# An attention layer and a bottleneck block in one kernel: other places for the residual's transfers, the weights' preparation and VectorE's share

## The chip, the cores and the metric

The kernel runs on one core of one Trainium2 chip. The metric is the device time of one execution in microseconds (us). A core has TensorE (PE), VectorE (DVE), ScalarE (ACT), GpSimd (POOL) and SyncE (SP). In the trace each engine runs its instructions in the order in which the program gives them to it. DMA transfers are issued on SP and on POOL here.

## The reference

The input x is (4, 1024, 32, 32) in float32: four images of 1024 channels and 1024 places. Layer 0 is attention with 16 heads of 64, layer 1 a bottleneck of three convolutions with batch norms.

```
x0 = tokens(x)                                    # (4, 1024, 1024)
q, k, v = split(x0 @ w_qkv.T + b_qkv)
q, k = rmsnorm(rope_2d(q)), rmsnorm(rope_2d(k))   # over all 1024 features
ctx = softmax(q @ k.T / 8) @ v                    # per head
x1 = rmsnorm(ctx @ w_proj.T) + x0                 # the residual
h = relu(bn(conv1x1(x1)))                         # 1024 -> 256
h = relu(bn(conv3x3(h)))                          # 256 -> 256
out = relu(x1 + softplus(s) * bn(conv1x1(h)))     # 256 -> 1024
```

## The kernel before

Everything is in float32. The images go through layer 0 one after another: projections q, k and v, attention, projection y. Layer 1 follows.

**Projections.** A 1024 x 1024 projection is a Strassen-like product (Winograd's form): seven products of halves instead of eight. Image 0 does this once (`project`, 28 steps); its operands are sums of weight blocks that `operands` makes on VectorE while TensorE works (L236 to L239: tiles such as w_v_1b) and stores to DRAM (wd, L242). Images 1 to 3, and y of all images, do it twice over (`project2`): seven outer products of seven inner ones, 49 weight tiles of 256 KB each, loaded on SP (L398, L465) into the ring wring of eight tiles. Their inner operands are sums of sums. `prepare` makes them once: four loads, four VectorE operations (L407 to L410), and four stores on POOL to wd2 (L412). A part is one of the seven outer products of one projection; there are 28 parts, and four block steps for y (`prepare_blocks`). Each part of q, k and v must be stored by the time image 1 projects, each of y by y of image 0.

**Where a part is prepared.** `weight_parts(parts, first, step, lag, alloc)` begins part i at `first + i * step` products from now, with its loads on POOL, and makes its sums `lag` products later. `alloc` gives room: pieces of a tile not yet in use (`pieces_of`), or `big_pieces`, which takes two tiles of the pool big (three tiles of 128 x 1024). Other parts are prepared in the attention of image 0: `extra_step` makes the sums of one part and loads the next, once per pair of heads, with loads on SP into wring. Before the change q of image 0 carries seven parts, k five, v none, attention the four block steps, y's seven parts and k's parts 2 to 6, and v's parts 2 to 5 are begun during y of image 0.

**Rope and norm.** `rope` turns q (and k) after its projection. The reciprocal norms are multiplied into the tables cosT and sinT (L722), and each of eight turns (L728 to L732) does two VectorE operations of 128 x 1024: one into a tile of big (qs or ks), one in place. Two accumulating transfers on POOL (L734) add the first into the second. The last turn reloads the tables (L169 to L172, on SP).

**Order.** For TensorE, VectorE, ScalarE and POOL the order is that in which the program issues, so a Python clock spreads VectorE's side work. Each product adds its share to `pace["room"]`; each piece of side work spends its cost in units of TT, VectorE's time for one operation of 128 x 512 as a share of a product. While room is left, `product_done` issues the next of `waiting`. A turn costs four TT. At the end of v `rest(leave=4)` leaves up to four turns in `waiting`, and attention issues one per pair. SP's order is found by a scheduler.

**Attention.** For each half c of the queries and each of eight pairs of heads: scores (L791), exponentials on ScalarE (L798), their sums over keys on VectorE (L800, L802), products with v (L808). Every second pair VectorE takes reciprocals (L835), which SP spreads (L838 and after), and POOL adds v's bias (L772). The tile probs_ holds one pair's exponentials.

**Residual.** `o_norm` writes the normed y to x1d in DRAM (L852). The residual is then added to x1d by eight accumulating transfers of 128 x 1024 on POOL (L1052) per image, issued all at once just before the next image's attention (for images 0 to 2; image 3 adds it on VectorE). x1d is read back after the last attention.

Of the kernel before, what the change touches and what calls it, by code (L numbers as in the profile page):

```python
# [13 lines left out]
ALU = mybir.AluOpType  # L14
# [4 lines left out]
P = 128  # L19
B, C, H, W = 4, 1024, 32, 32  # L20
N = H * W
NT = C // P
# [12 lines left out]
WQ, WK, WV, WP, W1 = 0, NFB, 2 * NFB, 3 * NFB, 4 * NFB  # L35
# [30 lines left out]
OUTER = ("A11", "A12", "S2", "S3", "S1", "S4", "A22")  # L66
# [19 lines left out]
def program(ctx, tc, x, wblk, w2, w3, vecs, cos, sin, out, bad):  # L86


    nc = tc.nc
# [6 lines left out]
    x1d = dram.tile([NT, P, B * N], F32, name=f"x1d{u}")  # L96
# [56 lines left out]
    with tc.tile_pool(name=f"st{u}", bufs=2) as st, ExitStack() as s:  # L153
# [70 lines left out]
        def operands(b, base, g, name):  # L224
# [14 lines left out]
            nc.vector.tensor_tensor(a12, a12, a11, ALU.subtract)  # L239
            spend(4 * TT)  # L240
            for o, t in enumerate((a11, s1, a21, a12)):
# [2 lines left out]

        TT = 0.19
        later, waiting = [], deque()
        pace = {"at": 0, "room": 0.0, "hold": False, "tables": 0.0}

        def spend(cost):
            pace["room"] -= cost
# [379 lines left out]
        def v_proj(b, bs, ts, v, two=None):  # L632

            if two is not None:
                project2(b, 1, WV, *two, v, True, "v", lambda c: None)
                return

            def outs(g):
                n = N // P // 2
                return [  # L640
                    v[:, c * n : (c + 1) * n, f * P : (f + 1) * P] for f in (g, g + NG) for c in range(NCH)
                ]

            project(b, WV, bs, ts, outs, None, lambda *a, **k: None, True, "v")
# [126 lines left out]
            nc.vector.tensor_tensor(cx, cx, w, ALU.mult)  # L771
            nc.gpsimd.tensor_scalar(cx, cx, col("bv", hp), None, ALU.add)  # L772

        def attention(b, c, q_all, k_all, v, probs_, late, ready, extra):


            at = half[c]
            sums_ = []
            for hp in range(NHP):
                n = f"{b}_{c}_{hp}"  # L780
                if late:
                    late.pop(0)()
                rows = shifts(q_all, k_all, n, hp, c) if bad is None else None
                probs = []
                d_ = acc.tile([P, 2, CH], F32, tag="tot", name=f"den_{n}")
                for t in range(N // P):
                    p = probs_[:, t]
                    sc = bank("sc", f"sc_{n}_{t}")
                    for j in range(2):
                        d = slice(j * HD, (j + 1) * HD)  # L790
                        nc.tensor.matmul(  # L791
                            sc[:, j], k_all[d, hp, t * P : (t + 1) * P], q_all[d, hp, at],
                            start=True, stop=bad is not None,
                        )
                    if bad is None:
                        for j in range(2):
                            nc.tensor.matmul(sc[:, j], ones[0:1, :], rows[j], start=False, stop=True)
                    nc.scalar.activation(p, sc, AF.Exp)  # L798
                    if t == 1:
                        nc.vector.tensor_tensor(d_, probs[0], p, ALU.add)  # L800
                    elif t > 1:
                        nc.vector.tensor_tensor(d_, d_, p, ALU.add)  # L802
                    probs.append(p)
                o = bank("cx", f"cx_{n}")
                for t in range(N // P):
                    for j in range(2):
                        h0 = (2 * hp + j) * HD
                        nc.tensor.matmul(  # L808
                            o[j * HD : (j + 1) * HD, :], v[:, t, h0 : h0 + HD], probs[t][:, j],
                            start=(t == 0), stop=(t == N // P - 1),  # L810
                        )

                nc.scalar.copy(q_all[:, hp, at], o)  # L813
                sums_.append(d_)
                if hp % 2 == 1:
                    for r in ready:
                        mean_of_v(q_all, *r)
                    ready.clear()
                if waiting:
                    next_waiting()  # L820
                elif extra:
                    extra.pop(0)()
                if hp % 2 == 0:
                    continue
                dn = bank("dn", f"dn_{n}")
                for i, d_ in enumerate(sums_):
                    for j in range(2):
                        q = slice((2 * i + j) * QH, (2 * i + j + 1) * QH)
                        nc.tensor.matmul(dn[q, :], ones[:, :QH], d_[:, j], start=True, stop=True)  # L829
                sums_ = []  # L830
                late.append(lambda *a, n=n, hp=hp, dn=dn: inverses(b, c, hp, n, dn, ready))
# [132 lines left out]
        def weight_parts(parts, first, step, lag, alloc):  # L964

            for i, (which, base, k) in enumerate(parts):

                def begin(which=which, base=base, k=k):
                    after(lag, prepare(which, base, k, alloc, nc.gpsimd))

                after(first + i * step, begin)

        def pieces_of(tile):

            at = deque(tile[:, i, h] for i in range(NT) for h in half)

            def alloc(name):
                at.rotate(-4)
                return [at[i] for i in range(-4, 0)]

            return alloc
# [15 lines left out]
        room = v_room("rq_0")  # L997
        for b in range(B):
            units = units_of(room)
            q_all = kv.tile([P, NT, N], F32, tag="q", name=f"q_{b}")  # L1000
# [6 lines left out]
            if b == 0:  # L1007
                unused = kp.tile([P, NT, N], F32, tag="k", name="unused")
                parts = [(which, base, k) for which, base in ((0, WQ), (1, WV)) for k in (0, 1, 6)]
                parts.append((3, WK, 0))  # L1010
                weight_parts(parts, 8, 2.7, 2.5, pieces_of(unused))
            tq = qk_proj(b, WQ, xs[b], ts[b], "bq", q_all, "q", w1 if b == 0 else None, two, True)
            rope(b, q_all, tq, eps_q, HD / C, None, "q", b == 0)
            k_all = kp.tile([P, NT, N], F32, tag="k", name=f"k_{b}")
# [1 line left out]
                ahead.append(two2[2][:2])  # L1016
            two = (3, *two2[1], False) if b > 0 else None
            if b == 0:
                parts = [(0, WQ, k) for k in (2, 3, 4, 5)] + [(3, WK, 1)]
                weight_parts(parts, 2, 4.5, 2.5, pieces_of(room))  # L1020
            tk = qk_proj(b, WK, xs[b], ts[b], "bk", k_all, "k", None, two)
            rope(b, k_all, tk, eps_rms, 1.0 / C, (wqk_other, wqk), "k")
            v = room
            v_proj(b, xs[b], ts[b], v, (*two2[2], False) if b > 0 else None)

            rest(leave=4 if b > 0 else 0)
# [3 lines left out]
            if b == 0:  # L1030
                todo = [lambda g=g: prepare_blocks(WP, g, pieces) for g in range(NG)]
                todo += [
                    lambda which=which, base=base, k=k: prepare(which, base, k, pieces)
                    for which, base, ks in ((2, WP, (0, 1, 6, 2, 3, 4, 5)), (3, WK, (2, 3, 4, 5, 6)))
                    for k in ks
                ]
            made = []
# [7 lines left out]
            extra = [extra_step] * len(todo)  # L1045
            if todo:
                extra_step()
            if b == B - 1:
                extra = filters()
            if b > 0:  # L1050
                for f in range(NT):
                    nc.gpsimd.dma_start(  # L1052
                        x1d[f, :, (b - 1) * N : b * N], x[b - 1, f * P : (f + 1) * P, :], accum_op=ALU.add
                    )
            late, ready = [], []
            probs_ = xp.tile([P, N // P, 2, CH], F32, tag="x", name=f"p_{b}")
            for c in range(NCH):
                attention(b, c, q_all, k_all, v, probs_, late, ready, extra)
            psum_for("proj")
            room = v_room(f"to_{b}")  # L1060
            tc_ = [
# [11 lines left out]
            if b + 1 < B:  # L1073
                xs[b + 1] = x_tile(b + 1)
                ts[b + 1] = t_tiles(b + 1)
                rows = (0, 1, 4, 5, 2, 3, 6, 7)
                for j in range(NT):

                    def load(b=b, i=rows[j]):
                        for c in range(NCH):  # L1080
                            load_x(b + 1, c, (i,))

                    after(3 + 1.5 * j, load)
                for i in range(0, NH, 2):

                    def queue(b=b, i=i):
                        waiting.append((7 * TT, lambda: sums(ts[b + 1], xs[b + 1], i)))

                    after(3 + 1.5 * (2 * i + 3) + 2, queue)
                if b == 0:  # L1090
                    weight_parts([(1, WV, k) for k in (2, 3, 4, 5)], 6, 7, 4, big_pieces)
            else:
                back = {1: x_tile(b + 1)}
                for i in range(NT):
                    after(8 + 1.5 * i, lambda i=i: read_back(1, (i,)))
# [252 lines left out]
        for f in range(NT):  # L1348
# [8 lines left out]
            for i, k in order:  # L1357
                b, c = divmod(i, NCH)
# [96 lines left out]
```

## Time and profile before

| | us |
|---|---|
| three runs of before | 2791.71, 2783.63, 2791.58 |
| their median | 2791.58 |
| the profiled execution | 2791.24 |
| its span on the core | 2789.4 |
| busy in the span: TensorE | 2702.7 |
| VectorE | 2127.9 |
| ScalarE | 1089.0 |
| GpSimd | 428.9 |

The granted clock of TensorE was 0.989 over the span. Times within the profile count from the span's start. The stages of layer 0, by TensorE's timeline: image 0 has q from 5.7 to 103.7, k to 209.7, v to 310.7, attention to 544.4, y to about 642.5; then q of image 1 to 728.0, k to 821.0, v to 920.9, attention to 1154.2, y to 1239.4; image 2 ends its v at 1514.7 and its attention at 1748.0; image 3's v runs from 2008.8 to 2117.7 and its attention to 2351.7. A line of the timeline gives start, duration, engine, line, operation, output <- input, shapes and count, and in brackets how long the engine stood before it and what ended that. A line of busy time by stage gives the stage's bounds and length, each engine's busy time with its count of instructions, TensorE's granted clock, the share of the 16 DMA engines in use, and GB/s.

### The profile page before, as it was taken

The page shows a single profiled execution, that of the slowest core. Times are in us where ns is not written, and L with a number is a line of the kernel's source. Part 1 is how long each engine was busy: PE and PEld are TensorE (multiplying, and loading weights), DVE is VectorE, ACT ScalarE, POOL GpSimd, SP SyncE. Part 2 cuts the span into 40 slices and gives each one's busy share as a digit, 9 for nine tenths or more (in the row PEclk, how much of TensorE's full clock was granted, in tenths as well). Part 3 has the DMA queues.
Part 4 walks back from the last instruction along what each step waited for, and adds up shares of the span by engine and source line. Part 5 has one row for each costly group of instructions (what it writes and reads, how often), then busy time and mean ns, then how long its engine had stood idle before and what let it go on. Part 6 is the DMA issues. An engine that isn't in the chain of part 4 may idle for free.

```text
span 2789.4 us, 33400 instructions
## 1 busy us (share of the span) xinstructions
PE 2702.7 (97%) x11914; PEld 1695.5 (61%) x11914; DVE 2127.9 (76%) x2461; ACT 1089.0 (39%) x1507; POOL 428.9 (15%) x511
## 2 busy tenths in 40 slices
PE   9999999999999999999999999999989999999997
PEld 4439633388878433588876333888874335846853
DVE  5565599988788677888886777887876877746987
ACT  2211455423342455333343555233424654312266
POOL 3453022221012010100111100100130111000000
PEclk9999999999999999999999999999999999999999
DMA  7896345587569300456777110665694002672165
GB/s 276 289 281 167 135 152 158 182 287 249 167 175 237 99 21 18 135 155 219 194 193 192 38 24 16 204 201 177 186 238 124 16 21 80 196 274 87 61 217 206
DMA packets 239168, 442.84 MB, mean 159 GB/s; under 512 B 27728, under 2 KB 112256, under 8 KB 238992
## 3 DMA queue, kind: packets, MB, share of 16 engines
q1 hardware_dynamic: 200496, 312.56, 35.5%
q0 software_dynamic: 38496, 128.05, 17.4%
q8 instruction: 97, 1.59, 0.2%
q14 instruction: 79, 0.65, 0.1%
HBM read 305.97 MB, written 96.78 MB: 144 GB/s over the span
## 4 chain that ended last, share of the span: by engine, by line
PE 81%; DVE 9%; DMA 6%; ACT 2%; issue 1%; SPq 0%; POOL 0%; DVEq 0%; POOLq 0%; ACTq 0%
PE sc L791 16%; PE cx L808 16%; PE p_y L478 9%; PE p_q L478 9%; PE p_v L473 7%; PE c L880 4%; PE c L1359 4%; PE p_k L478 3%; PE pa_v L312 2%; PE pa_q L304 2%; PE c2x L1218 1%; DMA w_v<-in_wblk_dram 1%; PE c2y L1218 1%; DMA w_v<-wdf 1%; PE dn L829 1%
## 5 line engine op out<-in xcount | busy, mean ns | idle before, releaser
L802 DVE TENSOR_TENSOR den<-den,p 128x1024 f32<-128x1024 f32 x384 | 470.4, 1225 | 41.1 <-DVE den L802 1.4
L798 ACT ACTIVATE p<-sc 128x1024 f32<-128x1024 f32 x512 | 476.1, 1043 | 64.8 <-PE sc L791 64.8
L791 PE MATMUL sc<-q,k 64*128 64x512 f32 x2048 | 457.2, 596 | 0.7 <-ACT rq L323 0.7
L791 PEld LDWEIGHTS sc<-q,k 64*128 64x128 f32 x2048 | 190.9, 186 | 265.0 <-issue 122.6
L808 PE MATMUL cx<-p,to 128*64 128x512 f32 x1536 | 340.2, 595 | 0.0
L808 PEld LDWEIGHTS cx<-p,to 128*64 128x64 f32 x1536 | 106.0, 137 | 228.3 <-issue 228.3
L772 POOL TENSOR_SCALAR q<-q,vec 128x512 f32<-128x512 f32 x64 | 126.8, 1988 | 637.4 <-DVE q L771 637.4
L478 PE MATMUL p_y<-q,w_y 128*128 128x256 f32 x928 | 210.7, 380 | 1.9 <-DMA w_y<-in_wblk_dram 1.7
L478 PEld LDWEIGHTS p_y<-q,w_y 128*128 128x128 f32 x928 | 175.3, 190 | 30.9 <-issue 6.3
L473 PE MATMUL p_v<-w_v,x 128*128 128x256 f32 x696 | 171.4, 402 | 20.4 <-DMA w_v<-wdf 8.4
L813 ACT COPY q<-cx 128x512 f32<-128x512 f32 x64 | 37.5, 587 | 357.2 <-PE cx L808 357.2
L473 PEld LDWEIGHTS p_v<-w_v,x 128*128 128x128 f32 x696 | 140.5, 203 | 44.4 <-issue 21.7
L478 PE MATMUL p_k<-to,w_k 128*128 128x256 f32 x672 | 154.7, 384 | 12.4 <-ACT to L566 9.4
L800 DVE TENSOR_TENSOR den<-p 128x1024 f32<-128x1024 f32 x64 | 76.6, 1196 | 111.4 <-ACT p L798 111.4
L478 PE MATMUL p_q<-to,w_q 128*128 128x256 f32 x672 | 154.2, 383 | 4.7 <-ACT q L532 4.6
L478 PEld LDWEIGHTS p_k<-to,w_k 128*128 128x128 f32 x672 | 127.8, 192 | 34.5 <-ACT to L566 11.8
L478 PEld LDWEIGHTS p_q<-to,w_q 128*128 128x128 f32 x672 | 128.4, 192 | 24.6 <-ACT q L532 5.9
L835 DVE RECIPROCAL rec<-dn 128x512 f32<-128x512 f32 x32 | 107.3, 3353 | 25.7 <-PE dn L829 25.6
L808 PE MATMUL cx<-p,rq 128*64 128x512 f32 x512 | 113.4, 595 | 0.0
L1359 PE MATMUL c<-h,w 128*128 128x512 f32 x256 | 110.3, 592 | 0.9 <-ACT h L1261 0.9
L734 POOL DMA_DIRECT2D k<-ks x64 | 54.8, 995 | 284.2 <-DVE k L728 159.1
L478 PE MATMUL p_y<-to,w_y 128*128 128x256 f32 x384 | 90.4, 380 | 0.8 <-DMA w_y<-wdf 0.7
(473 smaller groups left out, 4240.5 us busy)
## 6 DMA issues: line engine op xcount, KB each, us to landing
w_y<-wd2f SPq DMA_DIRECT2D x112, 256.0 KB
w_q<-wd2f SPq DMA_DIRECT2D x84, 256.0 KB
w_k<-wd2f SPq DMA_DIRECT2D x84, 256.0 KB
w_v<-wd2f SPq DMA_DIRECT2D x84, 256.0 KB
x<-in_x_dram SPq DMA_DIRECT2D x64, 256.0 KB
q<-qs POOLq DMA_DIRECT2D x64, 256.0 KB, 5.4
k<-ks POOLq DMA_DIRECT2D x64, 256.0 KB, 5.7
inv<-rec SPq DMA_DIRECT2D x256, 64.0 KB
```

The source lines that it names most:

```text
L304: nc.tensor.matmul(o, w[:, i, :], r(i), start=first and i == 0, stop=last and i == NH - 1, skip_group_check=True,)
L473: nc.tensor.matmul(o[:, q].rearrange("p (g f) -> p g f", g=2), r[:, i, q * P : (q + 1) * P], wt[:, :, i, :], skip_group_check=True, **at,)
L478: nc.tensor.matmul(o[:, q], wt[:, q, i, :], r[:, i, :], skip_group_check=True, **at)
L772: nc.gpsimd.tensor_scalar(cx, cx, col("bv", hp), None, ALU.add)
L791: nc.tensor.matmul(sc[:, j], k_all[d, hp, t * P : (t + 1) * P], q_all[d, hp, at], start=True, stop=bad is not None,)
L798: nc.scalar.activation(p, sc, AF.Exp)
L800: nc.vector.tensor_tensor(d_, probs[0], p, ALU.add)
L802: nc.vector.tensor_tensor(d_, d_, p, ALU.add)
L808: nc.tensor.matmul(o[j * HD : (j + 1) * HD, :], v[:, t, h0 : h0 + HD], probs[t][:, j], start=(t == 0), stop=(t == N // P - 1),)
L835: nc.vector.reciprocal(r, dn)
L880: nc.tensor.matmul(o, w[f][ih][:, ii, :], ys[:, i, half[c]], start=(i == 0), stop=(i == NT - 1))
L1359: nc.tensor.matmul(os[i], w3t[k][f // NH][:, f % NH, :], h2[b, k][:, half[c]], start=(k == 0), stop=(k == NPT - 1),)
```

## The change

1. TT, the cost of one VectorE operation in the pace, goes from 0.19 to 0.21.
2. The residual's eight transfers of the image before are no longer issued together ahead of attention. A list `slow` holds three empty steps and the eight transfers, and attention takes one per pair of heads.
3. The parts move. In image 0 q carries eight (k's part 6 is added; step 2.4 instead of 2.7, lag 4 instead of 2.5), k four (k's part 1 leaves; step 5, lag 4), v five (k's parts 1 to 5, in `big_pieces`, a step of 5.5 and a lag of 3.5). Attention of image 0 has the four block steps, y's seven parts and v's parts 2 to 5. None is begun behind attention.

```diff
-        TT = 0.19
+        TT = 0.21
...
-        def attention(b, c, q_all, k_all, v, probs_, late, ready, extra):
+        def attention(b, c, q_all, k_all, v, probs_, late, ready, extra, slow):
...
+                if slow:
+                    slow.pop(0)()
                 if waiting:
                     next_waiting()
                 elif extra:
...
-                parts.append((3, WK, 0))
-                weight_parts(parts, 8, 2.7, 2.5, pieces_of(unused))
+                parts += [(3, WK, k) for k in (0, 6)]
+                weight_parts(parts, 8, 2.4, 4, pieces_of(unused))
...
-                parts = [(0, WQ, k) for k in (2, 3, 4, 5)] + [(3, WK, 1)]
-                weight_parts(parts, 2, 4.5, 2.5, pieces_of(room))
+                parts = [(0, WQ, k) for k in (2, 3, 4, 5)]
+                weight_parts(parts, 2, 5, 4, pieces_of(room))
...
             v = room
+            if b == 0:
+                weight_parts([(3, WK, k) for k in range(1, len(OUTER) - 1)], 0.5, 5.5, 3.5, big_pieces)
             v_proj(b, xs[b], ts[b], v, (*two2[2], False) if b > 0 else None)
...
-                    for which, base, ks in ((2, WP, (0, 1, 6, 2, 3, 4, 5)), (3, WK, (2, 3, 4, 5, 6)))
+                    for which, base, ks in ((2, WP, (0, 1, 6, 2, 3, 4, 5)), (1, WV, (2, 3, 4, 5)))
...
-            if b > 0:
-                for f in range(NT):
-                    nc.gpsimd.dma_start(
-                        x1d[f, :, (b - 1) * N : b * N], x[b - 1, f * P : (f + 1) * P, :], accum_op=ALU.add
-                    )
             late, ready = [], []
+
+            def add_residual(f, b=b - 1):
+                nc.gpsimd.dma_start(
+                    x1d[f, :, b * N : (b + 1) * N], x[b, f * P : (f + 1) * P, :], accum_op=ALU.add
+                )
+
+            slow = [lambda: None] * 3 + [lambda f=f: add_residual(f) for f in range(NT)] if b > 0 else []
...
-                if b == 0:
-                    weight_parts([(1, WV, k) for k in (2, 3, 4, 5)], 6, 7, 4, big_pieces)
```

More of the change, by code (lines that the diff above doesn't have):

```diff
@@ L1049, in program @@
                 extra = filters()
-            if b > 0:
-                for f in range(NT):
-                    nc.gpsimd.dma_start(
-                        x1d[f, :, (b - 1) * N : b * N], x[b - 1, f * P : (f + 1) * P, :], accum_op=ALU.add
-                    )
-            late, ready = [], []
+            late, ready = [], []
+            def add_residual(f, b=b - 1):
[3 more added lines that the diff above has]
+            slow = [lambda: None] * 3 + [lambda f=f: add_residual(f) for f in range(NT)] if b > 0 else []
             probs_ = xp.tile([P, N // P, 2, CH], F32, tag="x", name=f"p_{b}")
             for c in range(NCH):
-                attention(b, c, q_all, k_all, v, probs_, late, ready, extra)
+                attention(b, c, q_all, k_all, v, probs_, late, ready, extra, slow)
             psum_for("proj")
```

## The prediction

> **What bounds the kernel now.** I read the page first, then busy time by stage, the waits of TensorE, its timeline where a stage is long, and VectorE's timeline in image 0. The page's engine row:
>
> ```profile
> PE 2702.7 (97%) x11914; PEld 1695.5 (61%) x11914; DVE 2127.9 (76%) x2461; ACT 1089.0 (39%) x1507; POOL 428.9 (15%) x511
> ```
>
> TensorE sets the time; nothing here changes its 11914 matmuls, so only its gaps, and the slow matmuls after them, can move. The stages (bounds, length, then busy us (count) of PE, PEld, DVE, ACT, POOL; clock, DMA share, GB/s) show where they are: k and v of image 0; attention 0, y 0 and q 1; k and v of image 1; attention 1; a clean q (image 2); v of image 3.
>
> ```profile
> 103.70:209.70 106.00, 99.41 (x233) 43.26 (x232) 64.66 (x82) 23.73 (x38) 51.71 (x78) 0.97 0.88 263
> 209.70:310.70 101.00, 101.00 (x905) 100.25 (x903) 44.57 (x50) 13.97 (x24) 23.50 (x34) 1.00 0.58 163
> 310.70:544.40 233.70, 233.03 (x1088) 84.42 (x1088) 212.78 (x195) 130.29 (x146) 58.86 (x73) 1.00 0.49 153
> 544.40:642.50 98.10, 90.19 (x412) 76.77 (x408) 88.50 (x113) 25.53 (x46) 25.19 (x34) 1.00 0.82 265
> 728.00:821.00 93.00, 87.84 (x403) 75.50 (x402) 75.20 (x97) 36.46 (x62) 11.42 (x14) 0.98 0.67 180
> 821.00:920.90 99.90, 91.30 (x402) 77.32 (x400) 74.76 (x91) 26.31 (x44) 21.80 (x26) 0.95 0.90 229
> 920.90:1154.20 233.30, 233.30 (x1089) 84.50 (x1089) 175.22 (x141) 128.42 (x144) 25.91 (x17) 1.00 0.12 27
> 1239.40:1324.90 85.50, 85.46 (x401) 74.32 (x400) 67.87 (x90) 30.14 (x51) 5.46 (x10) 1.00 0.64 205
> 2008.80:2117.70 108.90, 93.60 (x403) 79.07 (x401) 74.64 (x92) 25.14 (x44) 21.67 (x26) 0.92 0.87 223
> ```
>
> A projection of equal work takes 85.5 us clean, but v takes 99.9, 100.0 (image 2) and 108.9, with DMA at 0.9. Attention's DMA share is 0.12. TensorE's timeline at the end of v of image 1 names the cause:
>
> ```profile
> 898.76 2.38 PE L473 MATMUL p_v<-w_v,t 128*128 128x256 f32 x8 [2.32 <-DMA w_v<-in_wblk_dram]
> 900.94 8.38 PE L473 MATMUL p_v<-w_v,x 128*128 128x256 f32 x32
> 917.27 3.63 PE L473 MATMUL p_v<-w_v,x 128*128 128x256 f32 x8 [3.73 <-DMA w_v<-in_wblk_dram]
> ```
>
> Weights came late, just after eight residual transfers were issued together (from 886.3). Those transfers, from the page of L1052:
>
> ```profile
> DMA to landing us min/median/max: 10.0/19.0/27.9
> ```
>
> In image 0 the line to watch is VectorE's first wait for a turn's transfer, in v:
>
> ```profile
> 264.66 1.28 DVE L728 SCALAR_TENSOR_TENSOR ks<-k,wqk_other,sinT 128x1024 f32<-128x1024 f32 x1 [3.36 <-DMA k<-ks]
> ```
>
> The tiles "big" have three buffers: the seventh turn waits for the fourth's transfer.
>
> **The Trainium skill.** "DMA: Bandwidth & Descriptors", section "Issuing engines are not separate DMA queues": DMAs of all queues share 16 engines and interleave; agrees (POOL's residual delays SP's weights). "TensorE: Matmul & The Clock Gate", "What's actually happening": an idle window drops the array to half clock until it has been busy again; agrees (eight matmuls took 3.63 us after the wait, 1.89 otherwise). "Perfetto Trace Analysis", "Optimization Strategy": a gap that repeats can mean too few buffers for the next tile; the wait at 264.66 is one.
>
> **The change, part by part.** Against the profiled execution's 2791.24 us (span 2789.4 and 1.84 around it); the median of the runs shown, 2791.58, is 0.34 higher, so the same difference serves for it.
>
> *Residual into attention.* Eight 512 KB accumulating transfers per image go from the end of v to pairs 3 to 10, 14 us apart. The excess of v over 85.5 is 14.4, 14.5 and 23.4. In images 1 and 2 some 3.8 us of it came earlier (2.01 us of wait at 854.8, slow matmuls after it), when the tables' reload (1 MB), the broadcast of sums and turns met; that reload moves some 20 us later in SP's order, behind w_v_4_0, where SP may wait 3 to 4 us for q's last turn. Image 3 keeps its nine filter loads. I leave 1.5, 1.5 and 5: gain 44 (30 to 50). Price in attention: eight issues of about 0.8 us on POOL, busy 26 of 233; landings were 3.2 us apart, so 8 x 3.2 = 26 us of DMA in an idle stage: nothing. Behind them on POOL stand the last k turn's two transfers and L772. Without that cover a turn lands up to 10 us late, four pairs (56 us) before its use.
>
> *TT 0.21.* A turn (2 x 1.28 us) charges 0.84 instead of 0.76, so turns are issued later. In VectorE's order for images 1 to 3, four q turns instead of six stand before k's last block sums (L518), two of k's move from v into attention. At 808.2 TensorE waited 2.88 us for ScalarE, that for L518, with two turns just before: 5 us of work goes. Excess of k over 85.5: 7.5, 4.3, 4.3 = 16; gain 12 (5 to 15). In attention VectorE gains 4 x 2.56 us of work instead of 2 x 2.56, and two turns stand ahead of the first sum: 5 us late, recovered at 14.0 - 11.1 per pair; nothing, at worst 2 us an image.
>
> *Weight parts of WV from behind attention into it, those of WK out of it.* y 0 and q 1 lose four parts (4 VectorE operations of 0.69, 4 loads, 4 stores of 256 KB each). They take 183.6 against 170.7 in image 1 to 2: excess 12.9, from waits for VectorE's late reciprocal (2.39), w_y (1.70, 0.70) and q (4.59). Attention has 15 steps instead of 16, so its last pair has none and w_y_0 loads earlier. Gain 12 (8 to 13).
>
> *q and k of image 0.* WK 6 joins q (TensorE waits for nothing there, VectorE 56 of 103.7 busy: 0, at worst +5, since k's tile waits for its stores). WK 1 leaves k, lag 4 instead of 2.5: VectorE stood 6.4 to 8.7 us for loads ahead of w_k_2b, TensorE 6.06. The order still puts four turns ahead of w_k_2b, behind POOL's loads: gain 4 of 7 (0 to 7).
>
> *v of image 0: five parts of WK.* The DMA has room (0.58 share; 10 MB in 101 us brings 163 to some 260 GB/s, as in k), VectorE too (14 us on 44.6 of 101). The buffers have not. `big_pieces` takes two of "big"'s three; a part holds them from its loads to its stores. In VectorE's order part 3's tiles are taken before ks_3, and its sums come only behind ks_7 and w_v_2b. So ks_1 to ks_7 have one buffer: each waits for the transfer before it. Queued behind on VectorE: w_v_1b after ks_2, w_v_2b after ks_7; TensorE waits for these. One turn then costs 2.6 (two operations) + 0.5 (to POOL's issue) + 0.6 (second issue) + landing. Landing of these transfers was 3.2 to 10.7, median 5.7 for k. I take 5.0, as little else moves once TensorE stands: 8.7 us. From ks_0 at 32.4 us into v, ks_7 begins at 32.4 + 7 x 8.7 = 93.3, ends 95.9, and w_v_2b's first usable operand follows 2.1 later: 98.0. TensorE needs it at 65.1: **a stall of 33**, and 3 for slow matmuls after two stalls (w_v_1b is part of it, about 6): +36. With landings near 3.7 (7.4 a turn) +24; with 10.5 a turn +49.
>
> Sum: -44 - 12 - 12 - 4 + 36 = **-36**: 2755. Ends: gains 80 with +24 give -56, gains 50 with +49 give -1.
>
> **Rivals.**
> A. Slower. The same chain in v of image 0, with landings as long as at 155 to 168 us (8.6 to 10.4, behind part loads on POOL's queue): 12.8 a turn, ks_7 from 122, w_v_2b ready at 126.7, stall 61.6 + 3. With v of images 1 to 3 keeping 9 us each (gains 53) the sum is +12: 2803. It decides from the point where 7 x turn - 28 + 3 passes the gains: 11.1 us a turn at 53, 13.9 at 72. For: POOL carries those loads in the same stage. Against: most pairs landed in under 7.
> B. No stall in v of image 0: were turns issued earlier or buffers free, only the gains remain: 2791 - 72 = 2719. Against: the order above, and the wait at 264.66 with all three buffers.
> C. The residual was not v's limit: the tables' reload, moved towards its end, takes over, and v stays near 96. Gains 10 + 12 + 12 + 4 against 36: 2789. For: 2.01 us of wait came before any residual transfer. Against: the late weights at 898 to 917.
>
> **How the numbers follow.** Likeliest 0.59 (own range 2735 to 2790), A 0.18, B 0.10, C 0.13. A measurement of this kernel tells about 0.3% (8.4 us) from no change. Faster by more: nearly all of the first but 0.06, B, and 0.04 of C: 0.67. Same: 0.04 + 0.07 + 0.02 of A: 0.13. Slower: the rest, 0.20. The range from 2722 to 2802 leaves out half of A and half of B.
>
> **What would show it.** v of image 0 at 125 to 150 us with VectorE waiting at L728 for k<-ks seven times and TensorE for w_v_2b; v of images 1 to 3 at 87 to 92 with DMA near 0.65, attention still 233; k at 86; y and q after attention 0 near 171. Wrong if v of image 0 stays near 101 (B) or passes 160 (A), if v of image 1 stays above 95 (C), or if attention grows.

## Result, and the profile after

The changed kernel takes **2746.20 us** (median of 4 runs, 2745.29 to 2747.69) against 2787.79 us (4 runs, 2783.63 to 2791.71): ratio 0.9852, 95% interval 0.9831 to 0.9872. The prediction said 2755. The profiled execution took 2747.69 us, 43.6 less than the one of before; its span is 2745.9 us.

The page's engine row of the changed kernel shows the same 11914 matmuls, 97% become 98%, and VectorE's sum moved by 2.4 us: again only gaps and slow matmuls went.

```profile
PE 2683.1 (98%) x11914; PEld 1687.0 (61%) x11914; DVE 2130.3 (78%) x2461; ACT 1088.4 (40%) x1507; POOL 432.9 (16%) x515
```

Busy time by stage of the changed kernel, for the stages shown of before: k and v of image 0; attention 0, y 0 and q 1; k and v of image 1; attention 1; v of image 3. Columns are bounds, length, busy us (count) of PE, PEld, DVE, ACT and POOL, clock, DMA share, GB/s.

```profile
104.80:202.40 97.60, 97.16 (x233) 42.55 (x232) 64.31 (x81) 23.41 (x38) 50.25 (x76) 1.00 0.92 288
202.40:338.70 136.30, 106.41 (x907) 105.30 (x905) 58.41 (x70) 14.60 (x26) 46.33 (x70) 0.89 0.63 188
338.70:572.00 233.30, 233.30 (x1088) 84.41 (x1088) 213.02 (x195) 129.66 (x145) 59.36 (x73) 1.00 0.50 154
572.00:656.80 84.80, 84.80 (x397) 74.51 (x393) 75.55 (x94) 25.63 (x45) 7.84 (x4) 1.00 0.65 203
656.80:742.50 85.70, 85.66 (x402) 74.49 (x401) 68.08 (x91) 30.08 (x51) 5.44 (x10) 1.00 0.66 206
742.50:829.30 86.80, 86.04 (x402) 74.29 (x401) 70.27 (x92) 36.15 (x61) 7.98 (x10) 1.00 0.66 181
829.30:917.40 88.10, 85.92 (x401) 74.20 (x399) 69.79 (x88) 25.23 (x44) 11.42 (x14) 1.00 0.72 199
917.40:1150.90 233.50, 233.50 (x1090) 84.31 (x1089) 185.69 (x150) 129.71 (x145) 39.56 (x33) 1.00 0.26 55
1986.90:2074.80 87.90, 85.98 (x401) 74.21 (x400) 69.84 (x88) 25.27 (x44) 11.46 (x14) 1.00 0.79 217
```

Three things can be read here. The second row, v of image 0, is the one stage that grew much: 136.3 us with TensorE busy for 106.4 at a clock of 0.89. In images 1 to 3 every projection now lies within 3 us of the clean 85.5. And attention 1 carries the residual (DMA share 0.26 instead of 0.12) at an unchanged 233.5 us.

To compare kernels I bound every stage by the first matmul of it and of the next one. In these bounds the profiled executions differ as follows (us, before to after):

| stage | before | after | difference |
|---|---|---|---|
| q of image 0 | 98.0 | 99.3 | +1.3 |
| k of image 0 | 106.0 | 97.6 | -8.4 |
| v of image 0 | 101.7 | 136.3 | **+34.6** |
| y 0 and q 1 together | 183.2 | 170.5 | -12.7 |
| k of images 1, 2, 3 | 92.9, 89.8, 89.8 | 86.8, 86.8, 86.8 | -12.1 |
| v of images 1, 2, 3 | 100.1, 100.1, 108.9 | 88.1, 88.1, 87.9 | **-45.0** |
| all others | | | -1.2 |

Their sum is -43.5, the difference of the spans. So the net gain is some 79 us won and 36 us lost. The 1.3 in q of image 0 is within the scatter between runs: over all the runs of this document that stage took 97.8 to 99.3 us with the new parts and 98.0 to 99.1 with the old ones. VectorE's timeline of the changed kernel in v of image 0 shows the loss (start, duration, instruction, in brackets the idle time ahead of it and what ended it):

```profile
234.83 1.28 DVE L728 SCALAR_TENSOR_TENSOR ks<-k,wqk_other,sinT 128x1024 f32<-128x1024 f32 x1
242.75 1.28 DVE L728 SCALAR_TENSOR_TENSOR ks<-k,wqk_other,sinT 128x1024 f32<-128x1024 f32 x1 [5.32 <-DMA k<-ks]
251.99 1.28 DVE L728 SCALAR_TENSOR_TENSOR ks<-k,wqk_other,sinT 128x1024 f32<-128x1024 f32 x1 [3.86 <-DMA k<-ks]
259.97 1.28 DVE L728 SCALAR_TENSOR_TENSOR ks<-k,wqk_other,sinT 128x1024 f32<-128x1024 f32 x1 [1.39 <-DMA k<-ks]
271.48 1.28 DVE L728 SCALAR_TENSOR_TENSOR ks<-k,wqk_other,sinT 128x1024 f32<-128x1024 f32 x1 [8.90 <-DMA k<-ks]
279.11 1.28 DVE L728 SCALAR_TENSOR_TENSOR ks<-k,wqk_other,sinT 128x1024 f32<-128x1024 f32 x1 [5.03 <-DMA k<-ks]
286.74 1.28 DVE L728 SCALAR_TENSOR_TENSOR ks<-k,wqk_other,sinT 128x1024 f32<-128x1024 f32 x1 [5.03 <-DMA k<-ks]
294.38 1.28 DVE L728 SCALAR_TENSOR_TENSOR ks<-k,wqk_other,sinT 128x1024 f32<-128x1024 f32 x1 [5.04 <-DMA k<-ks]
```

All seven turns after the first wait for the transfer of the turn before. Two operand sums that TensorE needs, w_v_1b and w_v_2b, stand between and behind these turns in VectorE's order. TensorE's timeline of the same stage:

```profile
256.70 5.81 PE L312 MATMUL pa_v<-w_v_1b,t 128*128 128x128 f32 x32 [6.91 <-DVE w_v_1b L238]
299.10 6.75 PE L312 MATMUL pa_v<-w_v_2b,t 128*128 128x128 f32 x32 [22.30 <-DVE w_v_2b L238]
```

That is 29.2 us of waiting; the other 5.4 us of the 34.6 are longer matmuls (PE busy 106.41 in this stage, 101.00 before).

### The profile page after: what moved, and what is told of

It reads as the page before. It is cut to its first block, busy times and chain, and to the rows that moved or that the text cites. A ratio compares the mean times of both kernels' runs of the same rounds, so it can differ in the third digit from the quotient of the medians.

```text
span 2745.9 us, 33363 instructions
## 1 busy us (share of the span) xinstructions
PE 2683.1 (98%) x11914; PEld 1687.0 (61%) x11914; DVE 2130.3 (78%) x2461; ACT 1088.4 (40%) x1507; POOL 432.9 (16%) x515
## 4 chain that ended last, share of the span: by engine, by line
PE 83%; DVE 3%; DMA 3%; ACT 1%; issue 0%; POOL 0%; DVEq 0%; ACTq 0%
PE sc L791 16%; PE cx L808 16%; PE p_y L478 12%; PE p_q L478 9%; PE p_v L473 8%; PE p_k L478 7%; PE c L882 4%; PE c L1364 4%; DMA w_v<-wdf 2%; PE c2x L1223 2%; PE c2y L1223 1%; PE dn L831 1%; PE pa_v L312 1%; DMA k<-ks 1%; PE pc_v L312 1%
## 5 line engine op out<-in xcount | busy, mean ns | idle before, releaser
L798 ACT ACTIVATE p<-sc 128x1024 f32<-128x1024 f32 x512 | 476.2, 1043 | 53.7 <-PE sc L791 53.6
L808 PEld LDWEIGHTS cx<-p,to 128*64 128x64 f32 x1536 | 106.0, 137 | 228.2 <-issue 228.2
L473 PE MATMUL p_v<-w_v,x 128*128 128x256 f32 x696 | 157.8, 379 | 2.2 <-DMA w_v<-wdf 2.2
L473 PEld LDWEIGHTS p_v<-w_v,x 128*128 128x128 f32 x696 | 132.0, 190 | 21.2 <-PE p_v L473 3.4
L734 POOL DMA_DIRECT2D q<-qs x64 | 55.7, 1042 | 279.2 <-issue 179.9
```

The source lines that it names most:

```text
L473: nc.tensor.matmul(o[:, q].rearrange("p (g f) -> p g f", g=2), r[:, i, q * P : (q + 1) * P], wt[:, :, i, :], skip_group_check=True, **at,)
L734: nc.gpsimd.dma_start(dst[i::2, f, :], other[1 - i :: 2, :], accum_op=ALU.add)
L808: nc.tensor.matmul(o[j * HD : (j + 1) * HD, :], v[:, t, h0 : h0 + HD], probs[t][:, j], start=(t == 0), stop=(t == N // P - 1),)
```

## The experiments

Times are medians; ratios are to the kernel before, run in the same set on the same chip, with 95% intervals. Before took 2788.92, 2788.93 and 2792.66 us in the three sets. The changed kernel's 2746.20 comes from the first comparison. Where single stages are given they come from the profile of that run, in the bounds of the table, so from one execution each. They scatter: v of images 1 to 3 took 260.6 to 264.1 us together in the six runs that have TT 0.21 and no residual transfer in v. "The burst" is short for the eight residual transfers of an image issued together. In the code, `...` stands for what is left out, and an edit may be shortened.

### One part alone

**Only the residual (e1).** The kernel before, with the burst at L1052 replaced by one transfer per pair:

```
+ if slow: slow.pop(0)()            # in attention, behind each pair
- for f in range(NT): nc.gpsimd.dma_start(x1d[f, ...], x[b - 1, ...], accum_op=ALU.add)
+ slow = [lambda: None] * 3 + [lambda f=f: add_residual(f) for f in range(NT)]
```

> The kernel before with only the residual's transfers moved into attention, one per pair of heads. Theory (the burst at the end of v delayed v's weights): v of images 1, 2 and 3 falls from 100, 100 and 109 us to 87 to 90 each, DMA share there to about 0.65, k stays at 93, 90, 90, v of image 0 stays at 102, attention stays at 233; about 44 us less, 2744 us. Rival (the tables' reload and turns limit v, or two of k's turns that TT moves out of v do): v stays near 96, 10 us less, 2778 us.

Measured: 2752.90 us, ratio 0.9867 (0.9839 to 0.9895), 36 us less. v of images 1 to 3 took 90.8, 90.7 and 88.2: 39.4 less. k took 93.0, 91.5 and 92.7: 4.7 more, which no theory had said. The rival at 2778 is out. Whether the edit caused those 4.7 is open: the run "Place or spacing" below, with the same transfers in another spacing, has k 0.6 below the kernel before. TensorE is left with one wait for w_v in each of the three stages of v, 9.4 us in all; in image 1 it is 3.53 us at 857 us, well before the old burst.

**Only the share for turns (e2).** One number of the kernel before:

```
- TT = 0.19
+ TT = 0.21
```

> The kernel before with only TT 0.21. Theory: k of images 1 to 3 falls from 93, 90, 90 to about 87 each, 12 us less in all, v of images 1 to 3 unchanged near 100, 100, 109: 2776 us. Rival 1 (the turns that leave v are part of v's gain): v falls by 4 us an image too, 24 us less. Rival 2 (k's gain of the change came from elsewhere): within 3 us of before.

Measured: **2736.30 us**, ratio 0.9811 (0.9787 to 0.9835), 53 us less: more than the whole change brings, and none of the three expectations (the first rival had v's direction, but 4 us an image instead of 16). k of images 1 to 3 fell by 11.0, as the theory said; k of image 0 grew by 4.0. But v of images 1 to 3 fell as well, to 87.3, 87.4 and 86.7: 47.7 less, with all eight residual transfers still issued together at L1052. POOL's timeline at the end of v of image 1 tells why. In the kernel before the burst stands directly behind k's sixth turn (x2, x7 and x8 are instructions joined in one row):

```profile
885.19 1.74 POOL L734 DMA_DIRECT2D k<-ks  x2 [3.05 <-ACT to L566]
886.29 6.61 POOL L1052 DMA_DIRECT2D x1df<-in_x_dram  x7
```

With TT 0.21 alone it stands behind the fourth:

```profile
881.72 1.70 POOL L734 DMA_DIRECT2D k<-ks  x2 [18.33 <-ACT x L532]
886.95 1.71 POOL L734 DMA_DIRECT2D k<-ks  x2 [3.52 <-issue]
912.23 1.71 POOL L734 DMA_DIRECT2D k<-ks  x2 [23.57 <-ACT p L798]
914.74 1.71 POOL L734 DMA_DIRECT2D k<-ks  x2 [0.81 <-ACT p L798]
915.85 7.43 POOL L1052 DMA_DIRECT2D x1df<-in_x_dram  x8
```

v ended at 908.4. With TT 0.19 six of k's turns are issued within v, before its last block. With 0.21 only two are; the next two become due in the last block, where `pace["hold"]` is set, so they are issued behind v's last product. VectorE's timeline of this run has these two turns after v's end:

```profile
909.09 1.28 DVE L728 SCALAR_TENSOR_TENSOR ks<-k,wqk_other,sinT 128x1024 f32<-128x1024 f32 x1
910.41 1.28 DVE L728 SCALAR_TENSOR_TENSOR k<-k,wqk,cosT 128x1024 f32<-128x1024 f32 x1
911.61 1.28 DVE L728 SCALAR_TENSOR_TENSOR ks<-k,wqk_other,sinT 128x1024 f32<-128x1024 f32 x1
912.92 1.28 DVE L728 SCALAR_TENSOR_TENSOR k<-k,wqk,cosT 128x1024 f32<-128x1024 f32 x1
```

POOL's two transfers for each turn wait for VectorE, and the residual stands behind them on POOL's queue. (POOL's rows name ScalarE's L798 as what ended the wait; but both pairs begin 0.54 us after the end of their turn's second VectorE operation, as the pair at 881.72 does.) The burst starts at 915.85 instead of 886.29: after v.

**Only the weight parts (e3).** The kernel before plus the new places of the parts, that is, the changed kernel with

```
- TT = 0.21
+ TT = 0.19
- slow = [lambda: None] * 3 + [lambda f=f: add_residual(f) for f in range(NT)] if b > 0 else []
+ slow = []
+ if b > 0:
+     for f in range(NT): add_residual(f)
```

> The kernel before with only the weight parts placed anew (q, k and v of image 0, attention 0, none behind it); residual and TT as before. Theory (the parts' terms stand alone and add up with the others): v of image 0 at 136 (35 more), y 0 and q 1 together at 171 (13 less), k of image 0 at 98 (8 less), q 0 1 more; k and v of images 1 to 3 as before: about 15 us more, 2803 us. Rival (y 0 and q 1 gained by TT, not by the parts): they stay at 183, 28 us more, 2816 us.

Measured: 2806.15 us, ratio 1.0060 (1.0041 to 1.0079). v of image 0 took 132.4 (30.7 more), y 0 and q 1 170.5 (12.7 less): both terms belong to the parts, and the rival is out. k of image 0 stayed at 106.0, though its parts had the longer lag and were one fewer: that gain needs something else too. v of images 1 to 3 stayed long (99.4, 99.1, 107.0).

### Which edit removes v's delay

**The residual set back (e5).** The changed kernel, with all eight transfers ahead of attention again:

```
- slow = [lambda: None] * 3 + [lambda f=f: add_residual(f) for f in range(NT)] if b > 0 else []
+ slow = []
+ if b > 0:
+     for f in range(NT): add_residual(f)
```

> The changed kernel with the residual's eight transfers issued together ahead of attention, as before; TT 0.21 and the parts stay. New theory (TT 0.21 holds two of k's turns until after v's last product, and the burst stands behind them on POOL's queue, so it falls into attention anyway): the transfers are issued about 8 us after v's end, v of images 1 to 3 stays at 87 to 88, time within 3 us of the changed kernel's 2746 us. Theory of the prediction (the move of the residual itself brings v's gain): v back at 98 to 108, about 2790 us.

Measured: 2745.33 us, ratio 0.9846 (0.9827 to 0.9865), the same as the changed kernel. v stayed at 87.0, 88.1 and 87.0, and the first of the eight transfers was issued at 922.15, v having ended at 914.7. With TT 0.21 the residual's edit is worth nothing that these runs can tell.

**The burst put back into v (e6, e9).** The changed kernel, with the eight transfers issued in `turn`, right behind k's second turn, and none in attention; TT stays at 0.21:

```
  nc.gpsimd.dma_start(dst[i::2, f, :], other[1 - i :: 2, :], accum_op=ALU.add)
+ if f == 1 and tag == "k" and b > 0:
+     for g in range(NT): nc.gpsimd.dma_start(x1d[g, ...], x[b - 1, ...], accum_op=ALU.add)
```

> The changed kernel with the eight transfers issued together right behind k's second turn in v, some 67 us into the stage, where the kernel before had them (65 us); everything else as changed. Theory (the burst's time within v is what delays v's last weights): v of images 1 to 3 at 95 to 100, TensorE waits for w_v again, 24 to 40 us more than the changed kernel: 2770 to 2786 us. Rival (TT's fewer turns in v made the room, whatever the burst does): v stays at 87 to 90, 2746 to 2754 us.

Measured: 2763.13 us, ratio 0.9906 (0.9884 to 0.9928), 17 us more than the changed kernel: between the two expectations. v took 89.6, 92.2 and 97.5, 15.2 more in all. The burst began at 896.04, when SP had just started v's last row of four w_v loads (895.75). In the kernel before it began 3.3 us ahead of that row (886.29 and 889.56). That suggested the next run (e9), the same edit one turn earlier:

```
- if f == 1 and tag == "k" and b > 0:
+ if f == 0 and tag == "k" and b > 0:
```

> As the run before it with the residual in v, but the eight transfers one turn earlier, behind k's first turn in v, some 62 us into the stage. There the burst came 3.6 us later, measured against SP's last w_v loads, than in the kernel before; here it comes some 1.5 us earlier than in the kernel before. Theory (what counts is how many of v's last weight loads SP issues behind the burst): v of images 1 to 3 rises from 90, 92, 97 to 97 to 106, 20 us more than that run, about 2783 us. Rival (the rest of the old excess came from the six turns and the tables' reload in v): v stays within 2 us of that run, 2763 us.

Measured: 2783.90 us, ratio 0.9973 (0.9964 to 0.9983), on a chip where before took 2792.66. v took 98.1, 99.0 and 103.4: 36.4 more than in the changed kernel, with no edit but the place of these eight transfers. The chip is not the cause: a later run on the same one (e10) had 261.0 in v. SP's timeline of this run (its DMA issues) shows v's last seven weight loads in image 1:

```profile
891.49 2.10 SPq L398 DMA_DIRECT2D w_v<-in_wblk_dram  x2
894.94 11.52 SPq L465 DMA_DIRECT2D w_v<-wd2f  x4
908.90 0.38 SPq L398 DMA_DIRECT2D w_v<-in_wblk_dram  x1
```

POOL's timeline of this run shows the burst:

```profile
888.90 1.70 POOL L734 DMA_DIRECT2D k<-ks  x2 [18.87 <-ACT x L532]
890.00 7.42 POOL L737 DMA_DIRECT2D x1df<-in_x_dram  x8
```

The burst begins ahead of these seven loads of 256 KB, 4.9 us ahead of the row of four. That row takes 11.52 us to be issued (5.50 in e6 and in the kernel before). This is the stall passed on rather than its cause: each issue takes 0.3 us, and in between SP waits for TensorE at L473 (7.7 us in four waits), which gives the ring's tiles free, and for one earlier w_v load (3.6 us). TensorE's timeline of this run shows it waiting for those loads:

```profile
902.32 3.78 PE L473 MATMUL p_v<-w_v,t 128*128 128x256 f32 x8 [3.96 <-DMA w_v<-in_wblk_dram]
917.76 1.96 PE L473 MATMUL p_v<-w_v,t 128*128 128x256 f32 x8 [0.26 <-DMA w_v<-wd2f]
920.98 1.97 PE L473 MATMUL p_v<-w_v,t 128*128 128x256 f32 x8 [1.25 <-DMA w_v<-wd2f]
924.28 1.97 PE L473 MATMUL p_v<-w_v,x 128*128 128x256 f32 x8 [1.34 <-DMA w_v<-in_wblk_dram]
```

The Trainium skill, "DMA: Bandwidth & Descriptors", section "Issuing engines are not separate DMA queues", has the principle (queues share the engines), and the runs agree: POOL's transfers delay SP's. They add the size: some 5 us of earlier issue cost 21 us over three images (300.5 against 279.3 in v).

**Place or spacing (e7).** As e1, but with all eight transfers together at the fourth pair of attention:

```
- slow = [lambda: None] * 3 + [lambda f=f: add_residual(f) for f in range(NT)]
+ slow = [lambda: None] * 3 + [lambda: [add_residual(f) for f in range(NT)]]
```

> The kernel before with all eight residual transfers issued together at the fourth pair of attention; TT 0.19 and parts as before. Theory (the place counts, not the spacing; attention's DMA is idle): attention stays at 233, v of images 1 to 3 at 88 to 91 as with one per pair, about 2753 us. Rival (a burst holds up turns and VectorE in attention): attention grows by 1 us or more per image, or v is above 95.

Measured: 2752.36 us, ratio 0.9864 (0.9843 to 0.9885), as with one per pair (2752.90). Attention stayed at 233.4, 233.4 and 234.0; v took 90.7, 89.8 and 91.5. The place counts, the spacing does not.

### v and k of image 0

**The parts around the turns (e4).** The changed kernel; of the five WK parts two are begun before k's first turn and three after its last one, none between. The lag is 3 instead of 3.5; buffers, transfers and sums are the same.

```
- weight_parts([(3, WK, k) for k in range(1, len(OUTER) - 1)], 0.5, 5.5, 3.5, big_pieces)
+ for k, at in enumerate((0.5, 4.5, 15.5, 19.5, 23.5), 1):
+     weight_parts([(3, WK, k)], at, 0, 3, big_pieces)
```

> The changed kernel with the five WK parts in v of image 0 taken at other points: two before the first turn, three after the last, none between; number of parts, buffers and transfers unchanged. Theory (the turns waited because a part's tiles left them one buffer): VectorE no longer waits 4 to 9 us at L728 for k<-ks, TensorE no longer 22 us for w_v_2b, v of image 0 falls from 136 to 102 to 107; 30 to 34 us less, about 2714 us. Rival (five parts' 10 MB or VectorE's work is too much for this stage, wherever in it): v of image 0 stays above 120, 2730 us or more.

Measured: **2714.09 us**, ratio 0.9728 (0.9701 to 0.9755): 32 us less than the changed kernel. v of image 0 took 104.9. Its row of busy time by stage, between rounded bounds, shows TensorE back at full clock, at a higher DMA rate than in the stalled stage (233 GB/s instead of 188). The work is the same but for the last part's sums and stores: VectorE began those sums at 310.35, in attention, which took 233.4 (233.3 before):

```profile
202.00:307.00 105.00, 101.30 (x905) 100.27 (x905) 54.76 (x65) 14.83 (x26) 43.86 (x66) 1.00 0.79 233
```

Its turns run in groups of three, as three free buffers allow. VectorE's timeline of the fourth to the seventh:

```profile
246.75 1.27 DVE L728 SCALAR_TENSOR_TENSOR ks<-k,wqk_other,sinT 128x1024 f32<-128x1024 f32 x1
249.26 1.28 DVE L728 SCALAR_TENSOR_TENSOR ks<-k,wqk_other,sinT 128x1024 f32<-128x1024 f32 x1
251.78 1.28 DVE L728 SCALAR_TENSOR_TENSOR ks<-k,wqk_other,sinT 128x1024 f32<-128x1024 f32 x1
257.76 1.28 DVE L728 SCALAR_TENSOR_TENSOR ks<-k,wqk_other,sinT 128x1024 f32<-128x1024 f32 x1 [3.38 <-DMA k<-ks]
```

So neither the parts' traffic nor their sums were too much for the stage; the buffers that they held across the turns were. The edit also takes the parts' loads out from between the turns' transfers on POOL's queue, but that is the smaller share: in the changed kernel the last three turns, with nothing of a part between them, still took 7.6 us each, against 2.5 within a group here. Seven such turns are 53 of the 59.6 us that the seven took. A fourth buffer for "big" was not tried.

**The same without the residual's edit (e10).** The version of e4 with the edit of e5: the burst ahead of attention again.

> The changed kernel with the WK parts around the turns in v of image 0 and with the residual's transfers issued together ahead of attention as before. Theory (with TT 0.21 the residual's edit is worth nothing): within 3 us of the version with one transfer per pair, 2714 us. Rival (with v of image 0 repaired, the queues shift and the burst meets v's weights again): 2730 us or more.

Measured: 2715.92 us, ratio 0.9742 (0.9711 to 0.9773), the same within 3 us. So the best versions run have TT 0.21 and the parts around the turns, and the residual may stay where it was. The residual in attention and the parts around the turns with TT 0.19 were not run.

**The lag in k of image 0 (e8).** The changed kernel with the old step and lag in k, still with four parts:

```
- weight_parts(parts, 2, 5, 4, pieces_of(room))
+ weight_parts(parts, 2, 4.5, 2.5, pieces_of(room))
```

> The changed kernel with the step and lag of the parts in k of image 0 set back to 4.5 and 2.5 (their number stays at four). Theory (VectorE stood for parts' loads ahead of w_k_2b, and the longer lag removed that): k of image 0 rises from 98 to 104 to 108, 2752 to 2756 us. Rival (WK 1 gone from k, or the turns held by TT, made the gain): k stays at 97 to 99, 2746 us.

Measured: 2755.65 us, ratio 0.9879 (0.9857 to 0.9900). k of image 0 took 111.5. TensorE's timeline there:

```profile
171.70 5.72 PE L304 MATMUL pa_k<-t,w_k_2b 128*128 128x512 f32 x8 [5.61 <-DVE w_k_2b L238]
195.68 4.54 PE L304 MATMUL pa_k<-t,w_k_3b 128*128 128x512 f32 x6 [4.53 <-DVE w_k_3b L238]
```

VectorE stood 5.35 us for a part's load ahead of w_k_2b and 5.19 and 5.00 us for loads ahead of w_k_3b. With the longer lag but TT 0.19 (only the weight parts) the two waits were 3.70 and 3.20; with both edits 0.45 and none. Neither edit alone gives k's 8.4 us; TT alone costs k of image 0 4.0 (110.0).

## Why the prediction came out right, and where a step failed

**Residual into attention: 44 (30 to 50) predicted, v of images 1 to 3 gave 45.0.** The mechanism is shown: eight transfers ahead of the last weights cost 36.4 us when put there (e9), 39.4 less when taken away (e1). The price of nothing in attention held as well (233.3 to 233.5, in e1 and e7 too). But the step failed in *whose* gain it is. The prediction took the burst's place as fixed by its line, and changed by its edit alone. In the changed kernel TT 0.21 had moved it already: e5 gives the edit back at no cost. That this term fits the number is luck: the edit that it is booked to was worth nothing here. Had the change been TT alone, the prediction's terms would have said -12, and the chip says -53.

**TT 0.21: 12 (5 to 15) predicted, k of images 1 to 3 gave 12.1**, 11.0 of it with TT alone. The term's size was right; the step was incomplete. It saw two of k's turns go from v into attention. It missed that two more are held until v's last product is out, and it asked what stands behind the *residual* on POOL's queue, not what the residual stands behind. By TT alone v fell by 47.7, a little more than by any move of the residual (39.4): the sum came out only because either edit frees v, and the prediction counted v once. The few us that TT brings v beyond the residual's edit go, in image 1, with the wait of 3.53 us at 857 in e1. e9 points the same way: with the burst in v it still took 8.6 us less there than the kernel before. Whether fewer turns or the tables' later reload brought this, no run separates.

**Weight parts out of y 0 and q 1: 12 (8 to 13) predicted, 12.7 measured**, with the parts alone too (e3). The parts' leaving is shown as the cause; which of the waits that the prediction listed there gave how much was not tested.

**q and k of image 0: 4 (0 to 7) predicted, 7.1 measured** (8.4 in k, less 1.3 in q). The mis-sized term is the rest of the stall: the prediction left 3 of 7 us, the trace 0.45. (One line was read too widely: of its waits of 6.4 to 8.7 us "ahead of w_k_2b" only the 6.38 stands there; the 8.65 stands behind w_k_2b, ahead of w_k_3b.) It put the whole gain on the lag; e3 and e8 show that it takes the lag and TT together, as TT lets VectorE do w_k_1b one turn earlier (sums at 142.2 us, at 144.3 with TT 0.19).

**v of image 0: +36 (+24 to +49) predicted, +34.6 measured**, by the chain foretold. ks_0 began 32.4 us into v, ks_7 at 92.0 (93.3 foretold), w_v_2b's first operand was ready at 96.6 (98.0). A turn took 8.5 us on average against the 8.7 assumed, but not evenly: 11.5 for the one whose transfers were issued behind a part's four loads on POOL's queue, 7.6 for the last three, close to the 7.4 of the low end. That one long turn is the mechanism of rival A, once instead of seven times. The stall was 29.2 rather than 33, the slow matmuls 5.4 rather than 3. On the latter the runs agree with the Trainium skill, "TensorE: Matmul & The Clock Gate", section "What's actually happening", by which an idle window brings the array to half clock until it has been busy again: 32 matmuls took 5.81 and 6.75 us after the two stalls, 3.84 after one of 3.02 us in e4, and 3.74 without a stall. One sum of this term is off: +36 and +49 hold 3 us for slow matmuls and +24 does not; 7.4 us a turn gives +27 by the same working, and the sum's low end -53 instead of -56.

**The rivals.** A needed 11.1 us a turn and got 8.5. B's 2719 is what remains when the stall is taken away: e4 shows 2714 on the chip, by another placement rather than by more buffers. C is out by e9 and e1. Its sum doesn't fit its words either: v at 96 in all three images would be 21 us less, not 10.

Against the span's -43.5, the sum of -36 is short by 7.5: 3.1 in q and k of image 0, 1.4 in v of image 0, 1.1 in v and k of images 1 to 3, 0.7 in y 0 and q 1, and 1.2 in stages that the prediction did not price.

## What to carry to other kernels

Here the time at which a transfer was issued was set by what it stood behind on its queue: the same line came at 886.29 or at 915.85 us. Before pricing the move of a burst, follow what each of the other edits does to the instructions ahead of it, or a gain will be credited to the wrong edit. A scheduled job that holds a rotating buffer from load to store should not span another job that cycles through the same pool, where one engine does both in program order; placing the jobs one after the other brought 32 us here without any more memory. And where several edits are made together, run each alone: here the smallest was worth more (53 us less) than all three together (42 us less).

## What the runs showed that was not expected

- A change of 0.02 in the pace's cost moved a burst of 4 MB by 30 us on another engine's queue (886.29 to 915.85) and took 47.7 us off three stages.
- A few us in the burst's place count: with TT 0.21, begun 4.9 us ahead of the last row of four w_v loads (in image 1) it cost v 36.4 us over three images, begun 0.3 us behind that row's first issue 15.2, begun after v nothing. The lead alone does not set the cost: with TT 0.19 a lead of 3.3 us cost 39.4 (before against e1), and of the 15.2 us image 3 alone has 9.6, at the same lead as image 1.
- Eight accumulating transfers of 512 KB issued together cost attention nothing measurable (233.4 us), though the median from issue to landing in image 1 was 16.5 us in e5 against 8.8 with one per pair. In the trace "one per pair" left POOL in twos, about 29 us apart.
